# A selective scan on one core: a one-column softplus ahead of the softplus unit's projections, and unit 10 in another order

## The chip, the cores and the metric

The kernel runs on one core of a Trainium2 chip. The metric is the device time of one execution in microseconds, as the median of several runs. The core has five engines that run side by side, each through its own list of instructions in order: TensorE (PE, matmuls and transposes), VectorE (DVE), ScalarE (ACT, activation functions), GpSimd (POOL) and SyncE (SP, which issues most of the DMAs). They wait for one another by semaphores.

## The reference

The input is a batch of 8 images of 384 channels and 64 x 64 points, all fp32. Two layers are added to it one after the other. The first is a channel attention (group norm, 1x1 and 3x3 convolutions, an attention over channels, a projection). The second is a selective scan in four directions; nearly all of the time is spent there:

```python
xs = _cross_scan(x)                                   # 4 directions
x_dbl = jnp.einsum('bkdl,kcd->bkcl', xs, x_proj_weight)
dts, Bs, Cs = (x_dbl[:, :, :R], x_dbl[:, :, R:R + N], x_dbl[:, :, R + N:])
dts = jnp.einsum('bkrl,kdr->bkdl', dts, dt_projs_weight)
dt = jax.nn.softplus(dts + dt_projs_bias[None, :, :, None])
# for every position l, with 384 channels and N = 16 states:
dA = jnp.exp(dtt[..., None] * A)
h = h * dA + (dtt * ut)[..., None] * bt[:, :, None, :]
y = jnp.einsum('bkdn,bkn->bkd', h, ct)
```

The four directions' `y` are summed at the place where they belong, and a layer norm and a GELU follow.

## The kernel before

The images run one after the other. In an image the scan is cut into 32 *steps*: direction k (0 to 3) times eight chunks of 512 positions. A step is cut into 12 *units* r = 0 to 11: three blocks j of 128 channels times four groups g of NV = 4 states. So a unit is four scans of 128 channels x 512 positions, one for each state.

What one unit `u` passes through:

- `drive` (line 950, GpSimd): one product `db` of 128 x 2048 for the four states, from the weighted input `w` and the broadcast `B`. Three `db` buffers.
- `decay` (line 938, ScalarE): `da = exp(dt * A)` into PSUM, one for each state. The pool `ps_a` has three buffers under the tag `da`, so a decay has to wait for the scan three places back; the first projection `pd` of a burst (below) takes its turn in the same three.
- `scan` (line 962, VectorE): `h = da * h + db` along the 512 positions, four to a unit.
- `turn` (line 983, TensorE): four transposes of 128 x 128 into one PSUM tile `pt`; a unit has four such groups. The pool `ps_t` has two buffers, shared with two of the projections.
- `keep` (line 989, ScalarE): the copy `hc` of one `pt` to SBUF.
- `add_up` (line 1000, TensorE): four matmuls that sum the states, weighted with C, into `py`.
- `take` (lines 1040 and 1042, VectorE): adds a finished `py` to the sum of the directions, which SyncE then stores.

The order of all these is written out by hand in `unit(u)` (line 1079), and `pin` keeps it: each engine gets its instructions in the order of the calls. The unit's scans run beside the transposes, copies and sums of the unit before it (`o = u - 1`), and two decays of the next unit are made ahead. `turned(lb)`, `scanned(v)`, `kept(lb)`, `added(lb)` are the calls for one quarter of a unit. The quarter 3 of `add_up` is called one unit later (`added(3, o - 1)`).

In unit 9 of every step but the last of an image the next step's step sizes are made. The code calls it `burst`; there are 31 in an image, 248 in all. TensorE makes three projections `pd` (line 904, `step_matmul`), ScalarE takes the softplus of each (line 912, `step_size`), and VectorE spreads C into four tiles (line 889, `spread_c`). Softplus and exp lie in different activation tables, so ScalarE loads a table ahead of the first softplus and another ahead of the next exp. The burst's own order is:

```python
take(s, 0)
pd0 = step_matmul(s + 1, 0)
kept(1)
pd1 = step_matmul(s + 1, 1)
pd2 = step_matmul(s + 1, 2)
added(0)
for j, pd in enumerate((pd0, pd1, pd2)):
    step_size(s + 1, j, pd)
```

Then come the scans 2 and 3, a decay, `spread_c`, `take(s, 1)`, `added(1)`, `turned(2)`, another decay, `kept(2)`, `turned(3)`, `kept(3)`, `added(2)`. In units 10 and 11 the usual order returns. In unit 10 GpSimd also makes the first `w` (line 921, `weigh`) from the new step size.

The SBUF pools of the scan are `wp` (weights and constants) and, laid behind it, `work` (all tiles that turn over: `B`, `db`, `w`, `dt`, `h`, `hc`, `cp`, the sums).

Of the kernel before, what the change touches and what calls it, by code (L numbers as in the profile page):

```python
# [9 lines left out]
F32 = mybir.dt.float32  # L10
AF = mybir.ActivationFunctionType
# [4 lines left out]
P = 128  # L16
# [79 lines left out]
def tile_channel_attention_then_selective_scan(ctx: ExitStack, tc: tile.TileContext, a: dict):  # L96
    nc = tc.nc
# [19 lines left out]
    small = {}  # L117
# [662 lines left out]
    def selective_scan(b, x1, stats1, after):  # L780

        y_d = dram.tile([L, C], F32, tag="yd", bufs=2, name=f"yd{b}")
        with ExitStack() as st:
            wp = st.enter_context(tc.tile_pool(name=f"sw{b}", bufs=1, reuse_waits="tile"))
# [5 lines left out]
            pin = tc.keep_in_program_order  # L790
# [30 lines left out]
            def view(t, k, c):  # L821

                if k % 2 == 0:
                    return t[:, bass.ts(c, CH)].rearrange("p (x y) -> p x y", y=W)
                return t.rearrange("p (h w) -> p w h", w=W)[:, bass.ts(c, CH // H), :]

            def split(t):
                return t.rearrange("p (x y) -> p x y", y=W)
# [63 lines left out]
            def fetch(s, g):  # L892

                bts[s, g] = work.tile([P, NV, CH], F32, tag="B", bufs=NG, name=f"B{b}_{s}_{g}")
                nc.sync.dma_start(
                    bts[s, g], bc_ds[s][NV * g : NV * (g + 1), :].partition_broadcast(P)
                )

            def step_matmul(s, j):

                k = steps[s][0]
                pool, tag = (ps_a, "da") if j == 0 else (ps_t, "t")
                pd = pool.tile([P, CH], F32, tag=tag, name=f"pd{b}_{s}_{j}")
                pin(nc.tensor.matmul(  # L904
                    pd, lhsT=wdt[:, k, bass.ts(j, P)], rhs=xds[s], start=True, stop=True
                ))
                return pd

            def step_size(s, j, pd):
                k = steps[s][0]  # L910
                dts[s, j] = work.tile([P, CH], F32, tag="dt", bufs=4, name=f"dt{b}_{s}_{j}")
                pin(nc.scalar.activation(  # L912
                    dts[s, j], pd, AF.Softplus, bias=small["dt_bias"][:, j, k : k + 1]
                ))

            def weigh(s, j):

                k, c = steps[s][:2]
                eng = nc.vector if s == 0 else nc.gpsimd
                ws[s, j] = work.tile([P, CH], F32, tag="w", bufs=3, name=f"w{b}_{s}_{j}")  # L920
                pin(eng.tensor_mul(split(ws[s, j]), view(x1[j], k, c), split(dts[s, j])))  # L921
# [3 lines left out]
            def place(u):  # L925

                s, r = divmod(u, UN)
                return s, *divmod(r, NG)

            def decay(i):  # L930

                u, v = divmod(i, NV)
                if u >= U:
                    return
                s, j, g = place(u)
                n = NV * g + v
                t = ps_a.tile([P, CH], F32, tag="da", name=f"da{b}_{u}_{v}")
                pin(nc.scalar.activation(  # L938
                    t, dts[s, j], AF.Exp, scale=neg_a[:, j, steps[s][0], n : n + 1]
                ))  # L940
                das[i] = t
# [11 lines left out]
            def scan(u, v):  # L953
                s, j, g = place(u)
                k, c, start, end = steps[s]
                n = NV * g + v
                if v == 0:
                    hs[u] = work.tile([P, CH, NV], F32, tag="h", bufs=3, name=f"h{b}_{u}")
                da, db, h = das.pop(NV * u + v), dbs[u][:, v, :], hs[u][:, :, v]
                if k >= 2:  # L960
                    da, db, h = da[:, ::-1], db[:, ::-1], h[:, ::-1]
                pin(nc.vector.tensor_tensor_scan(  # L962
                    h, da, db, 0.0 if start else carries[s - 1][:, j, n : n + 1],
                    ALU.mult, ALU.add,
                ))
# [12 lines left out]
            def turn(u, lb):  # L978

                t = ps_t.tile([P, NF, P], F32, tag="t", name=f"pt{b}_{u}_{lb}")  # L980
                for f in range(NF):
                    q = NF * lb + f
                    pin(nc.tensor.transpose(t[:, f, :], hs[u][:, bass.ts(q, HP), :].rearrange("p l v -> p (l v)"), ident))  # L983
                pts[u, lb] = t

            def keep(u, lb):

                t = work.tile([P, NF, P], F32, tag="hc", bufs=6, name=f"hc{b}_{u}_{lb}")
                pin(nc.scalar.copy(t, pts.pop((u, lb))))  # L989
                hcs[u, lb] = t  # L990
# [39 lines left out]
            def sum_of(s, j):  # L1030

                sums[s, j] = work.tile([P, NLB, P], F32, tag="ysum", bufs=3, name=f"ys{b}_{s}_{j}")
                if steps[s][0] > 0:
                    move_y(s, j, sums[s, j], False)
# [13 lines left out]
            for j in range(NJ):  # L1048
                step_size(0, j, step_matmul(0, j))
                weigh(0, j)  # L1050
            for g in range(1, NG):
                fetch(0, g)
            mingle_c(0)
# [25 lines left out]
            def unit(u):  # L1079

                o = u - 1
                s, r = divmod(u, UN)
                nxt = s + 1 < S
                last = u == U
                burst = r == 9 and nxt
                i0 = NV * u

                def scanned(v):
                    if not last:
                        scan(u, v)  # L1090

                def turned(lb):
                    if o >= 0:
                        turn(o, lb)

                def kept(lb):
                    if o >= 0:
                        keep(o, lb)

                def added(lb, of=o):  # L1100
                    if of >= 0:
                        add_up(of, lb)

                if r in (2, 6, 10) and not last:
                    sum_of(s, r // 4)
                if not nxt and r in (8, 10) and not last:
                    take(s, (r - 8) // 2)
                if r >= 8 and nxt:
                    fetch(s + 1, r - 8)

                if not last:
                    drive(u + 1)
                if u >= 2:
                    keep_last(u - 2)
                if r == 7 and nxt:
                    mingle_c(s + 1)
                if r == 10 and nxt:
                    weigh(s + 1, 0)
                if 0 < s < S and r in (0, 2):
                    weigh(s, 1 + r // 2)  # L1120

                turned(0)
                scanned(0)
                added(3, o - 1)
                if r == 4 and s > 0 and not last:
                    take(s - 1, 2)
                decay(i0 + 2)
                kept(0)
                turned(1)
                if r == 8 and nxt:  # L1130
                    turn_c(s + 1)
                scanned(1)
                decay(i0 + 3)
                if burst:
                    take(s, 0)
                    pd0 = step_matmul(s + 1, 0)
                    kept(1)
                    pd1 = step_matmul(s + 1, 1)
                    pd2 = step_matmul(s + 1, 2)
                    added(0)  # L1140
                    for j, pd in enumerate((pd0, pd1, pd2)):
                        step_size(s + 1, j, pd)
                    scanned(2)
                    scanned(3)
                    decay(i0 + 4)
                    for g in range(NG):
                        spread_c(s + 1, g)
                    take(s, 1)
                    added(1)
                    turned(2)  # L1150
                    decay(i0 + 5)
                    kept(2)
                    turned(3)
                    kept(3)
                    added(2)
                    return
                kept(1)
                if nxt and r < 4:
                    for i in range(3):
                        project(s + 1, 3 * r + i)  # L1160
                turned(2)
                added(0)
                scanned(2)
                decay(i0 + 4)
                kept(2)
                turned(3)
                added(1)
                if r == 4 and nxt:
                    lay_out(s + 1)
                scanned(3)  # L1170
                decay(i0 + 5)
                kept(3)
                added(2)
# [136 lines left out]
```

## Time and profile before

| | |
|---|---|
| median of 3 runs | 19440.91 us (19436.96 to 19442.3) |
| the profiled execution | 19452.52 us |
| its span, first to last instruction | 19450.7 us |
| TensorE's mean granted clock | 0.958 |
| VectorE busy | 18413.2 us |
| ScalarE busy | 17504.7 us |
| TensorE busy | 17034.3 us |
| GpSimd busy | 16881.1 us |
| a decay `da`, busy | 713 ns, 12288 of them |
| a copy `hc`, busy | 605 ns, 12288 of them |
| a scan `h` with a carry, busy | 1263 ns, 10752 of them |
| a product `db`, busy | 4581 ns, 3072 of them |
| a table load, busy | 1283 ns, 256 ahead of softplus and 256 ahead of exp in line 938 |

A row of the groups is read so: line, engine, operation, output <- inputs, how many; then busy time and the mean of one in ns; then the engine's idle time just before them and what ended it. A row of the waits is: who <- for whom: us in all, how many times, the longest. A row in order of time is: start, length, engine, line, operation, how many in a row, and in brackets the idle time before it and what ended it. Instructions of one engine follow each other a little closer than their lengths, since they overlap at the ends. TensorE's clock is given as a share of full speed; it is either 1 or one half at a time.

### The profile page before, as it was taken

What the parts mean: (1) busy time and instruction counts of PE and PEld (TensorE: products, weight loads), DVE (VectorE), ACT (ScalarE), POOL (GpSimd) and SP (SyncE); (2) the same over time, 40 slices, a digit from 0 to 9 for tenths busy, and PEclk for the clock granted to TensorE, in tenths of its full rate; (3) what the DMA queues carried; (4) which work ended last, traced back from release to release, by engine and by line L of the source; (5) the groups of instructions that cost most, each with busy time, mean ns of one, the idle gap of its engine ahead of it and who ended that gap; (6) DMA issues with size and microseconds to landing.
All of it is one profiled execution on the core that took longest, in us unless ns stands there. A gap on an engine that the chain in (4) does not pass through costs nothing.

```text
span 19450.7 us, 414947 instructions
## 1 busy us (share of the span) xinstructions
PE 17034.3 (88%) x166560; PEld 10177.3 (52%) x166560; DVE 18413.2 (95%) x17526; ACT 17504.7 (90%) x29605; POOL 16881.1 (87%) x7486
## 2 busy tenths in 40 slices
PE   7888888888888888888888888888888888888887
PEld 4555545555455554555545555455554555545554
DVE  8999989999899998999989999899998999989998
ACT  6999979999799997999979999799997999979998
POOL 4999959999599995999959998599985999869997
PEclk9999999999999999999999999999999999999998
DMA  1232332223322232222322322323223222222323
GB/s 57 85 98 98 101 101 81 97 98 102 103 86 92 96 107 98 87 95 93 103 98 87 98 98 96 104 82 97 98 96 108 83 94 97 96 94 89 98 94 120
DMA packets 1204102, 1849.23 MB, mean 95 GB/s; under 512 B 154656, under 2 KB 1019168, under 8 KB 1064960
## 3 DMA queue, kind: packets, MB, share of 16 engines
q1 hardware_dynamic: 1201312, 1822.57, 28.6%
q8 instruction: 1314, 21.53, 0.5%
q14 instruction: 612, 5.01, 0.1%
q10 hardware_dynamic: 864, 0.12, 0.0%
HBM read 1503.58 MB, written 318.77 MB: 94 GB/s over the span
## 4 chain that ended last, share of the span: by engine, by line
ACT 37%; PE 33%; DVE 18%; issue 6%; POOL 4%; DMA 1%; SPq 0%; DVEq 0%; ACTq 0%; POOLq 0%
ACT da L938 15%; PE pt L983 14%; ACT hc L989 14%; DVE h L962 12%; PE py L1000 7%; PE px L847 5%; DVE ac L457 4%; POOL db L950 4%; ACT dt L912 2%; PE pp L603 2%; ACT pr L419 1%; PE pd L904 1%; PE py L1006 1%; ACT L912 1%; ACT L938 1%
## 5 line engine op out<-in xcount | busy, mean ns | idle before, releaser
L950 POOL TENSOR_TENSOR db<-w,B 128x2048 f32<-128x2048 f32 x3072 | 14061.9, 4581 | 464.6 <-DVE h L962 438.7
L962 DVE TENSOR_TENSOR_SCAN h<-da,ca,db 128x512 f32<-128x512 f32 x10752 | 12783.8, 1263 | 296.6 <-ACT da L938 273.8
L938 ACT ACTIVATE da<-dt,neg_a 128x512 f32<-128x512 f32 x12288 | 8748.9, 713 | 33.5 <-DVE h L962 29.8
L983 PE MATMUL pt<-ident,h 128*128 128x128 f32 x49152 | 8097.9, 293 | 699.3 <-DVE h L962 436.3
L989 ACT COPY hc<-pt 128x512 f32<-128x512 f32 x12288 | 7403.7, 605 | 702.8 <-PE pt L983 644.9
L983 PEld LDWEIGHTS pt<-ident,h 128*128 128x128 f32 x49152 | 5432.6, 145 | 3150.4 <-issue 1877.1
L1000 PE MATMUL py<-hc,cp 128*32 128x128 f32 x98304 | 5061.3, 289 | 897.8 <-ACT hc L989 725.8
L1000 PEld LDWEIGHTS py<-hc,cp 128*32 128x32 f32 x98304 | 2043.3, 109 | 3161.1 <-ACT hc L989 1622.4
L962 DVE TENSOR_TENSOR_SCAN h<-da,db 128x512 f32<-128x512 f32 x1536 | 1749.1, 1206 | 102.3 <-ACT da L938 89.9
L426 POOL TENSOR_TENSOR pr<-pr,pr 128x1008 f32<-128x1008 f32 x288 | 673.1, 2337 | 1194.8 <-ACT pr L419 1172.8
L847 PE MATMUL px<-x,wx 128*44 128x128 f32 x6144 | 1212.9, 341 | 82.1 <-DVE cp L889 68.2
L921 POOL TENSOR_TENSOR w<-x,dt 128x512 f32<-128x512 f32 x744 | 1059.8, 1424 | 27.0 <-ACT dt L912 24.9
L847 PEld LDWEIGHTS px<-x,wx 128*44 128x44 f32 x6144 | 683.7, 127 | 409.9 <-issue 235.2
L904 PE MATMUL pd<-xd,wdt 128*128 128x512 f32 x1536 | 729.3, 611 | 155.8 <-DVE h L962 149.7
L432 POOL TENSOR_TENSOR pr<-pr,pr 128x1008 f32<-128x1008 f32 x288 | 574.8, 1996 | 237.0 <-ACT pr L419 173.2
L603 PE MATMUL pp<-v,mT 128*128 128x512 f32 x1152 | 547.1, 623 | 100.1 <-DVE v L462 99.1
L889 DVE TENSOR_TENSOR cp<-quad,pct 128x512 f32<-128x512 f32 x1024 | 628.0, 674 | 0.0
L976 POOL COPY ca<-h 128x4 f32<-128x4 f32 x2688 | 539.0, 201 | 0.0
L912 ACT ACT_TABLE_LOAD x256 | 328.4, 1283 | 226.2 <-PE pd L904 225.2
L904 PEld LDWEIGHTS pd<-xd,wdt 128*128 128x128 f32 x1536 | 271.4, 190 | 462.6 <-issue 235.2
L912 ACT ACTIVATE dt<-pd,dt_bias 128x512 f32<-128x512 f32 x768 | 474.8, 685 | 6.6 <-PE pd L904 2.9
L1042 DVE TENSOR_TENSOR ys<-ys,py 128x512 f32<-128x512 f32 x576 | 383.7, 666 | 34.6 <-PE py L1000 34.6
(335 smaller groups left out, 11320.2 us busy)
## 6 DMA issues: line engine op xcount, KB each, us to landing
B<-bcd SPq DMA_DIRECT2D x1024, 1024.0 KB, 4.8
yd<-ys SPq DMA_DIRECT2D x384, 256.0 KB, 3.3
ys<-yd SPq DMA_DIRECT2D x768, 128.0 KB, 2.8
yd<-ys SPq DMA_DIRECT2D x768, 128.0 KB, 4.3
x<-in_x SPq DMA_DIRECT2D x48, 1024.0 KB, 7.5
x1d<-x SPq DMA_DIRECT2D x192, 256.0 KB, 3.0
ys<-yd SPq DMA_DIRECT2D x192, 256.0 KB, 2.9
fy<-yd SPq DMA_DIRECT2D x128, 384.0 KB, 4.0
```

Of the source, the lines that this page charges most:

```text
L457: pin(nc.vector.scalar_tensor_tensor(o, pre[:, r0 + dy - lo : r1 + dy - lo, x0 + dx : x1_ + dx], weight(t, tap), o, ALU.mult, ALU.add,))
L603: pin(nc.tensor.matmul(pps[m, c], lhsT=fold_of[0][:, j, bass.ts(m, P)], rhs=vs["v"][:, j, bass.ts(c, CH)], start=j == 0, stop=j == NJ - 1,))
L847: pin(nc.tensor.matmul(split(pxs[s][:XR, :])[:, part, :], lhsT=wx[:, j, k, :], rhs=view(x1[j], k, c)[:, part, :], start=i == 0, stop=i == ...
L904: pin(nc.tensor.matmul(pd, lhsT=wdt[:, k, bass.ts(j, P)], rhs=xds[s], start=True, stop=True))
L912: pin(nc.scalar.activation(dts[s, j], pd, AF.Softplus, bias=small["dt_bias"][:, j, k : k + 1]))
L921: pin(eng.tensor_mul(split(ws[s, j]), view(x1[j], k, c), split(dts[s, j])))
L938: pin(nc.scalar.activation(t, dts[s, j], AF.Exp, scale=neg_a[:, j, steps[s][0], n : n + 1]))
L950: pin(eng.tensor_mul(t, w.broadcast_to([P, NV, CH]), bts[s, g]))
L962: pin(nc.vector.tensor_tensor_scan(h, da, db, 0.0 if start else carries[s - 1][:, j, n : n + 1], ALU.mult, ALU.add,))
L983: pin(nc.tensor.transpose(t[:, f, :], hs[u][:, bass.ts(q, HP), :].rearrange("p l v -> p (l v)"), ident))
L989: pin(nc.scalar.copy(t, pts.pop((u, lb))))
L1000: pin(nc.tensor.matmul(py[f * HP : (f + 1) * HP, lb, :], lhsT=cps[s, g][:, q, :], rhs=hc[:, f, :], start=g == lb == 0, stop=g == NG - 1 an ...
```

## The change

The burst gets one more ScalarE instruction: a softplus of one column of the constant `dt_bias`, into a one-column tile `warm` that nothing reads. It stands between the copy 1 and the second projection in the calls, so on ScalarE it is ahead of the three softplus. The tile is taken from the pool `wp`, once for each image.

In unit 10 of every step the fourth decay (`i0 + 3`) is called right behind the third, ahead of the copies 0 and 1. The sum `added(2)` at the end of the burst moves into unit 10, behind its `turned(0)` and ahead of `added(3, o - 1)`, where it is called with `o - 1` and so is still the sum of the same unit.

```diff
@@ -1048,6 +1048,7 @@
                 weigh(0, j)
+            warm = wp.tile([P, 1], F32, name=f"warm{b}")
             for g in range(1, NG):
@@ -1120,21 +1121,27 @@
                 turned(0)
+                if r == 10 and nxt:
+                    added(2, o - 1)
                 scanned(0)
                 added(3, o - 1)
                 if r == 4 and s > 0 and not last:
                     take(s - 1, 2)
                 decay(i0 + 2)
+                if r == 10:
+                    decay(i0 + 3)
                 kept(0)
                 turned(1)
                 if r == 8 and nxt:
                     turn_c(s + 1)
                 scanned(1)
-                decay(i0 + 3)
+                if r != 10:
+                    decay(i0 + 3)
                 if burst:
                     take(s, 0)
                     pd0 = step_matmul(s + 1, 0)
                     kept(1)
+                    pin(nc.scalar.activation(warm, small["dt_bias"][:, 0, 0:1], AF.Softplus))
                     pd1 = step_matmul(s + 1, 1)
                     pd2 = step_matmul(s + 1, 2)
                     added(0)
@@ -1152,7 +1159,6 @@
                     kept(2)
                     turned(3)
                     kept(3)
-                    added(2)
                     return
```

## The prediction

> **What bounds the kernel now.** I read the page first: the busy shares, then the waits, then one step of the scan in order of time.
>
> ```profile
> PE 17034.3 (88%) x166560; PEld 10177.3 (52%) x166560; DVE 18413.2 (95%) x17526; ACT 17504.7 (90%) x29605; POOL 16881.1 (87%) x7486
> ```
>
> and the groups of instructions, where the figure after the second bar is ScalarE's idle time before them:
>
> ```profile
> L912 ACT ACT_TABLE_LOAD x256 | 328.4, 1283 | 226.2 <-PE pd L904 225.2
> ...
> L938 ACT ACT_TABLE_LOAD x256 | 328.4, 1283 | 4.5
> ```
>
> VectorE is at 95%, so what can be won is at most its idle time. The waits say for whom it idles:
>
> ```profile
> POOL db L950 <- DVE h L962: 438.7, 288, 4.6
> ...
> DVE h L962 <- ACT da L938: 363.7, 824, 2.4
> ...
> ACT L912 <- PE pd L904: 225.2, 217, 1.8
> ```
>
> VectorE loses 363.7 us to decays (`da`) that ScalarE has not made yet. There are 8 images x 31 bursts (unit 9 of a step, where the next step's step sizes are made) = 248, so 1.47 us a burst. GpSimd waits for VectorE, not the reverse: it stands one to two units ahead until its three `db` buffers are full. ScalarE idles 225.2 us before the softplus table load, for the first projection. Where in a step this falls is seen in the order of time; this is one burst of a step with direction 0:
>
> ```profile
> 3163.94 0.59 ACT L989 COPY hc<-pt 128x512 f32<-128x512 f32 x1
> 3165.58 1.28 ACT L912 ACT_TABLE_LOAD   x1 [1.05 <-PE pd L904]
> 3166.87 1.84 ACT L912 ACTIVATE dt<-pd,dt_bias 128x512 f32<-128x512 f32 x3
> 3168.73 1.28 ACT L938 ACT_TABLE_LOAD   x1
> 3170.03 1.30 ACT L938 ACTIVATE da<-dt,neg_a 128x512 f32<-128x512 f32 x2
> 3171.27 1.05 ACT L989 COPY hc<-pt 128x512 f32<-128x512 f32 x2
> 3172.22 0.70 ACT L938 ACTIVATE da<-dt,neg_a 128x512 f32<-128x512 f32 x1
> 3172.95 0.59 ACT L989 COPY hc<-pt 128x512 f32<-128x512 f32 x1
> 3173.43 0.70 ACT L938 ACTIVATE da<-dt,neg_a 128x512 f32<-128x512 f32 x1
> 3174.57 0.58 ACT L989 COPY hc<-pt 128x512 f32<-128x512 f32 x1 [0.45 <-PE pt L983]
> ```
> ```profile
> 3169.55 0.68 DVE L1040 COPY ys<-py 128x512 f32<-128x512 f32 x1
> 3170.82 4.81 DVE L962 TENSOR_TENSOR_SCAN h<-da,ca,db 128x512 f32<-128x512 f32 x4 [0.59 <-ACT da L938]
> 3175.84 3.67 DVE L962 TENSOR_TENSOR_SCAN h<-da,ca,db 128x512 f32<-128x512 f32 x3 [0.21 <-issue]
> ```
>
> Counted from the softplus load at 0: the copy before it ends at -1.05, the three softplus run 1.30 to 3.14, the exp load 3.15 to 4.44, the first decay 4.45 to 5.14. VectorE was free at 4.65 and starts the scan at 5.24: 0.59 lost, the same in nearly every burst. More is lost near 8.9 and 10.1, where decays 3 and 4 of unit 10 and after are late: they stand behind copies (`hc`) that wait for TensorE's transposes (`pt`). By position, counted over the 248 bursts in the trace, VectorE loses 145 us at 4 to 6 us after the load, 118 us at 6 to 12, and 104 us later.
>
> The rest of the step shows what the wait costs. Two steps, one without and one with half-clock time of TensorE in it:
>
> ```profile
> 4580.00:4641.40 61.40, 54.77 (x611) 32.00 (x612) 60.74 (x56) 58.26 (x103) 60.83 (x29) 1.00 0.30 97
> 3165.60:3227.80 62.20, 54.74 (x620) 34.14 (x619) 60.91 (x56) 58.89 (x103) 60.01 (x29) 0.97 0.25 85
> ```
>
> (The columns: length; busy PE, weight load, DVE, ACT, POOL; clock; DMA.) VectorE is busy 60.7 to 60.9 us in both, and the length is that plus its idle: 0.6 and 1.3 us. So a microsecond of wait removed shortens the step by one, down to a floor of about 60.9, where GpSimd's own work (60.0 with directions 0 and 2, 60.8 with 1 and 3) comes in.
>
> **The change, part by part.** *The one-column softplus.* It adds 248 ScalarE instructions and no load: in the built order the table load moves from the first softplus to this one, and loses its wait for TensorE. Its price: the 128x3 square roots of line 166 took 204 ns; the bounds are 0.19 (a one-column accumulator read on ScalarE) and 0.69 (a 512-column softplus); I take 0.20, since three columns are next to one. The load now runs -1.03 to 0.25, the small one to 0.45, and the first softplus starts there instead of at 1.30. The second and third wait for their projections: TensorE's last pass of the third ends at 1.63, so with 0.08 us to be seen the third starts at 1.71 instead of 2.45 and ends at 2.40 instead of 3.14. All behind it gains 0.74. In bursts that already have no wait (the 31 of 248 whose load waited 0 to 0.1, mostly the first of a direction) it costs up to 0.2.
>
> A rule speaks against this. The Trainium skill (ScalarE: Activation LUTs, What ACT_TABLE_LOAD costs) gives a switch 1283 ns for the load and some 1380 ns of drain. The load agrees with the row; but the exp load starts 0.02 us after the third softplus ends, and 256 of them have 4.5 us idle in all before them, so the row has no drain. By the rule the early load would run 0.33 to 1.61 and softplus start at 1.81, 0.51 later than now: 248 x 0.51 = 126 us lost. I take the row.
>
> *Decay 3 ahead of the copies in unit 10, and the sum moved.* No instruction is added. Decay 3 needs a PSUM buffer that scan 0 of unit 10 frees: it may wait there, with copies 0 and 1 (unit 9's transposed states) behind it, and TensorE's third transpose group behind copy 0. The moved sum (`py`, four matmuls, 0.35 us of TensorE's issue by the distance 3171.89 to 3172.25 in the trace) no longer stands ahead of unit 9's first transposes. No DMA moves; the orders of VectorE, GpSimd and SyncE stay as they were. The eight last steps of an image get the reordering without a burst; there the copy is at most one scan (1.2 us) late, behind two buffered transposes: nothing.
>
> *Walk after both* (same zero, durations and pitches of the rows): exp load 2.42 to 3.70; decay 0 to 4.40, so scan 0 starts at 4.57 right behind the sum on VectorE (pitch 0.09 under its end): 0.59 gone. Decay 1 to 5.01, two copies to 6.01, decay 2 to 6.60, decay 3 to 7.2 (scan 0 has ended at 5.86, no wait). Scans 2 and 3 are due at 6.95 and 8.13: both ready. Copies 0 and 1 at 7.12 and 7.60 if TensorE is at full clock (its transposes run from 5.57; the second group, behind the moved sum and the next, ends near 7.5). Decay 4 ends at 8.78, scan 4 is due at 9.31: 0.5 to spare.
>
> *TensorE's clock takes part back.* In the trace's clock record, 222 of 248 bursts are followed by half clock for 3.4 or 6.8 us, starting 5.0 to 8.5 after the load, after a TensorE pause of 2.47 us (3.85 to 6.32). After the change the pause lasts from about 3.55 (third softplus earlier) to 5.57: 2.0 us, shorter, so it comes somewhat less often but not never. With half clock from 5.57 on, four transposes take 1.12 instead of 0.66 and four `py` 0.65 instead of 0.43 (both in the trace), the second group ends at 8.9, decay 4 at 10.1: 0.87 lost; with half clock from 6.8 on, nothing. The Trainium skill (TensorE: Matmul & The Clock Gate, Part 1) has the clock decided by a free-running window of 3413 ns; the trace's half-clock starts do lie on one such grid. Then 18 windows are 61.44 us. A burst that lies badly makes a step of 60.85 + 0.87 = 61.7, one that lies well 60.9; the one slides the burst later against the grid, the other earlier, so steps tend to settle near the edge between, at 61.44 on average. By the rule 0.6 us a burst stay; by the rows alone, with a burst anywhere on the grid, about 0.35. I take 0.6, as the trace has runs of steps of 61.43 already.
>
> **Sum.** 363.7 us of wait now; after it 248 x 0.6 = 149: 215 us saved. The profiled execution took 19452.5 us (span 19450.7), 11.6 over the median 19440.9: 0.06%, left out. 19441 - 215 = **19226 us**, -1.1%.
>
> **Rivals.** (1) *The clock stays up*: with a shorter pause and no settling, 0.2 a burst remain: 363.7 - 50 = 314 saved, **19127**. For: 26 bursts have no half clock now. Against: a pause of 2.0 us is still more than half a window. (2) *Half clock nearly always, and early*: 222 bursts keep 0.87 + 0.25 (late waits): 247 stay, 117 saved, **19324**. (3) *No change*: GpSimd takes VectorE's place, **19441**. Against: over the steps it is busy 60.4 us of 62.4, and the floor that I use is above that. (4) *Slower through addresses*: the small tile stands ahead of the scan's work tiles, so in the built program `B`, `db`, `w`, `dt`, `h`, `hc` and the sums lie 32 bytes further, off the 64-byte multiples they had. Were GpSimd's 12 products a step dearer by 5% (4.58 to 4.81 us), it would be busy 60.4 + 2.8 = 63.2 and bound the step: +1 us x 248, **19690**. It decides from 0.15 us (3%) a product on. Against: tiles that lie at 32 now cost the same (softplus to an aligned tile 0.688, line 374's bias to one at 32 0.687; GpSimd's 768-element product at 32 took 1.82, on the line between its 512 at 1.28 and 2048 at 4.58). No row has these very operations at 32.
>
> **How the numbers follow.** Forecast 0.60 (19180 to 19290), (1) 0.14, (2) 0.13, (3) 0.04, (4) 0.09. A range from 19105 to 19350 holds the first three. Faster by over 0.2% (39 us, about what this measurement can tell) 0.87, within it 0.04, slower 0.09.
>
> **What would show it.** Right: the wait for `pd` before the load gone and 248 one-column softplus near 0.2 us; the 0.59 gap before unit 10's first scan gone; the decay wait of VectorE near 150; `db` at 4.58 us as before. Wrong: idle time between copy and load (a drain); a small softplus over 1 us, from where the early load gains nothing; gaps moved to scan 4 or 5; longer products on GpSimd.

## The result and the profile after

The changed kernel takes 19267.62 us (median of 4 runs, 19259.11 to 19273.3) against 19441.6 us before, measured beside it: 174.0 us less, ratio 0.9908 with a 95% interval of 0.9893 to 0.9922. The forecast was 19226 (19180 to 19290). The profiled execution took 19266.71 us (span 19264.9).

First the instructions of the new line of the kernel after (line 1144).

```profile
L1144 ACT ACT_TABLE_LOAD  x248: 1283/1283/1283, 496.5 to 19087.0; - x124
L1144 ACT ACTIVATE warm<-dt_bias x248: 202/203/206, 497.8 to 19088.3; 128x1 f32<-128x1 f32 x124
```

(Here min/median/max of one in ns, then first and last start.) The table load belongs to the small softplus now, and that softplus takes 203 ns. No row shows a wait ahead of either. Three rows of the waits of the kernel after, then the row of the same name as the last of them in the kernel before:

```profile
POOL db L950 <- DVE h L962: 270.7, 244, 4.5
...
DVE h L962 <- ACT da L938: 147.0, 352, 2.1
...
DVE h L962 <- issue: 65.4, 104, 1.1
```
```profile
DVE h L962 <- issue: 16.5, 52, 0.8
```

VectorE's wait for decays fell from 363.7 to 147.0 us, and ScalarE's 225.2 us ahead of the table load are gone from the list (the softplus themselves now wait 22.0 us for projections). But the scans' row "issue" (nothing that the profile shows) had 16.5 us before and has 65.4 now. A decay has ended less than 0.5 us before each of these 104 scans; I take them for the same wait under another name, which the profile does not show outright. One burst of the kernel after in order of time, from the load on:

```profile
3141.43 0.59 ACT L989 COPY hc<-pt 128x512 f32<-128x512 f32 x1
3142.04 1.28 ACT L1144 ACT_TABLE_LOAD   x1
3143.33 0.20 ACT L1144 ACTIVATE warm<-dt_bias 128x1 f32<-128x1 f32 x1
3143.44 2.05 ACT L912 ACTIVATE dt<-pd,dt_bias 128x512 f32<-128x512 f32 x3
3145.51 1.28 ACT L938 ACT_TABLE_LOAD   x1
...
3149.00 1.31 ACT L938 ACTIVATE da<-dt,neg_a 128x512 f32<-128x512 f32 x2
3150.23 0.59 ACT L989 COPY hc<-pt 128x512 f32<-128x512 f32 x1
3151.07 0.59 ACT L989 COPY hc<-pt 128x512 f32<-128x512 f32 x1 [0.25 <-PE pt L983]
```
```profile
3147.03 0.70 DVE L1040 COPY ys<-py 128x512 f32<-128x512 f32 x1
3147.63 7.17 DVE L962 TENSOR_TENSOR_SCAN h<-da,ca,db 128x512 f32<-128x512 f32 x6
3154.96 1.29 DVE L962 TENSOR_TENSOR_SCAN h<-da,ca,db 128x512 f32<-128x512 f32 x1 [0.16 <-ACT da L938]
3156.73 2.46 DVE L962 TENSOR_TENSOR_SCAN h<-da,ca,db 128x512 f32<-128x512 f32 x2 [0.48 <-ACT da L938]
```

The load starts 0.02 us after the copy. The 0.59 us gap behind `ys` has gone: six scans run without a gap where it was four behind a gap. The waits that are left in this burst come in unit 11, behind copies of ScalarE that wait for transposes (`0.25 <-PE pt`). TensorE is then at half clock, as two stretches of the same burst show (length; busy PE, weight load, DVE, ACT, POOL; clock; DMA):

```profile
3148.00:3150.00 2.00, 1.32 (x21) 0.88 (x22) 2.00 (x3) 2.00 (x5) 2.00 (x1) 0.93 0.93 286
3150.00:3152.00 2.00, 2.00 (x12) 1.43 (x16) 2.00 (x3) 1.75 (x4) 1.17 (x2) 0.50 0.66 197
```

Half clock follows a pause of TensorE. The row that ends the pause, in the prediction's burst of the kernel before and in the burst above:

```profile
3171.89 0.43 PE L1000 MATMUL py<-hc,cp 128*32 128x128 f32 x8 [2.47 <-ACT hc L989]
```
```profile
3148.68 0.66 PE L983 MATMUL pt<-ident,h 128*128 128x128 f32 x4 [2.37 <-ACT hc L989]
```

Counted in the clock record, half clock that begins 4 to 10 us after the load follows 199 of the 248 bursts, against 222 before.

### The profile page after: what moved, and what is told of

Its sections match the earlier page's. It is cut to its first block, busy times and chain, and to the rows that moved or that the text cites. A ratio compares the mean times of both kernels' runs of the same rounds, so it can differ in the third digit from the quotient of the medians.

```text
span 19264.9 us, 415195 instructions
## 1 busy us (share of the span) xinstructions
PE 16919.5 (88%) x166560; PEld 10165.1 (53%) x166560; DVE 18369.1 (95%) x17526; ACT 17529.4 (91%) x29853; POOL 16878.7 (88%) x7486
## 4 chain that ended last, share of the span: by engine, by line
ACT 38%; PE 36%; DVE 19%; issue 5%; DMA 1%; POOL 0%; SPq 0%; DVEq 0%; ACTq 0%; POOLq 0%
ACT da L938 17%; ACT hc L989 15%; PE pt L983 14%; DVE h L962 13%; PE py L1000 7%; PE px L847 5%; DVE ac L457 3%; PE pd L904 3%; PE pp L603 2%; ACT pr L419 2%; PE py L1006 1%; ACT L938 1%; ACT dt L912 1%; ACT ac L419 1%; DVE acc L462 1%
## 5 line engine op out<-in xcount | busy, mean ns | idle before, releaser
L950 POOL TENSOR_TENSOR db<-w,B 128x2048 f32<-128x2048 f32 x3072 | 14064.4, 4582 | 296.1 <-DVE h L962 270.7
L1000 PE MATMUL py<-hc,cp 128*32 128x128 f32 x98304 | 4990.3, 288 | 284.5 <-ACT hc L989 115.0
L603 PEld LDWEIGHTS pp<-v,mT 128*128 128x128 f32 x1152 | 219.1, 198 | 358.7 <-issue 232.3
```

Of the source, the lines that this page charges most:

```text
L603: pin(nc.tensor.matmul(pps[m, c], lhsT=fold_of[0][:, j, bass.ts(m, P)], rhs=vs["v"][:, j, bass.ts(c, CH)], start=j == 0, stop=j == NJ - 1,))
L950: pin(eng.tensor_mul(t, w.broadcast_to([P, NV, CH]), bts[s, g]))
L1000: pin(nc.tensor.matmul(py[f * HP : (f + 1) * HP, lb, :], lhsT=cps[s, g][:, q, :], rhs=hc[:, f, :], start=g == lb == 0, stop=g == NG - 1 an ...
```

## The experiments

Each is timed against the kernel before on its own chip; three chips took part in the experiments, and the kernel before had medians of 19430 to 19445 us on them. A step below is the time from one softplus table load to the next; "ordinary" steps leave out those next to a change of direction or beside the work for the next image (144 of them in a run). Medians are in us; the ratio is to the kernel before.

| kernel | median | ratio, 95% interval | half clock after bursts | mean ordinary step |
|---|---|---|---|---|
| before | 19441.6 | 1 | 222 | 62.25 |
| the change | 19267.62 | 0.9908 (0.9893 to 0.9922) | 199 | 61.46 |
| softplus alone | 19250.85 | 0.9897 (0.9883 to 0.9912) | 170 | 61.46 |
| reordering alone | 19412.24 | 0.9984 (0.9976 to 0.9992) | 202 | 62.15 |
| tile of 64 bytes | 19259.83 | 0.9901 (0.9887 to 0.9916) | 205 | 61.45 |
| change + filler | 19066.12 | 0.9802 (0.9785 to 0.9818) | 0 | 60.66 |
| softplus + filler | 19082.23 | 0.9816 (0.9799 to 0.9832) | 0 | 60.76 |
| before + filler | 19217.23 | 0.9884 (0.9869 to 0.9899) | 0 | 61.40 |
| change + short filler | 19154.82 | 0.9859 (0.9844 to 0.9873) | 119 | 61.00 |

### The two parts apart

The softplus alone is the kernel before with two lines; the reordering alone is the changed kernel without them.

```diff
+            warm = wp.tile([P, 1], F32, name=f"warm{b}")
...
                     kept(1)
+                    pin(nc.scalar.activation(warm, small["dt_bias"][:, 0, 0:1], AF.Softplus))
```

> The one-column softplus alone; unit 10 in its old order, the sum back at the burst's end. Theory A (waits removed, and steps that settle on TensorE's clock grid): the 0.59 us gap ahead of unit 10's first scan goes, a step without half clock falls from 61.43 to about 60.8 us, one with it stays near 61.6, so steps gather at 61.44: 150 to 180 us saved, 19260 to 19290. Rival B (waits removed, one for one): 0.59 x 248 = 146 saved, but the later gaps (118 us at 6 to 12 us after the load) all stay and the rest of the measured gain belongs to the reordering: 19295 to 19320.

> Unit 10's order and the moved sum alone, no softplus and no extra tile. The 0.59 gap stays in both theories. Theory A: a step without half clock stays at 61.43, which is as good as 18 windows of 3.413 us, a step with it falls from 62.2 to 61.8 or so; steps drift to the places without half clock and stay there: 80 to 140 saved, 19300 to 19360, and the savings of the two parts alone add up to clearly more than the 174 of both together. Rival B: only what the softplus alone leaves of the 174: 20 to 40 saved, 19400 to 19420, and the two add up to 174.

Softplus alone: 193 us saved, as much as the whole change or a little more (the intervals overlap), and 13 more than theory A allowed; rival B, with 149 at most, misses by more. Reordering alone: 32 us saved. The sum of the two, 225, is more than the 174 of both, as theory A said, but A had 80 to 140 for the reordering, and its reason fails: the reordering by itself did not send the steps to places without half clock (202 bursts with it, ordinary steps of 62.15). Its 32 us are in rival B's range, and beside the softplus it is worth nothing that these runs can tell. Where VectorE's scans wait, in us over the 248 bursts and by the time from the softplus load to the start of the wait, says why:

| us after the load | before | softplus alone | reordering alone | the change |
|---|---|---|---|---|
| 4 to 6 | 145 | 30 | 144 | 27 |
| 6 to 9.7 | 43 | 25 | 0 | 0 |
| 9.7 to 12.2 | 76 | 41 | 99 | 85 |
| 12.2 to 17 | 41 | 43 | 41 | 51 |

The second row is the wait before scan 3 of unit 10, the third the wait before the first scan of unit 11. The early decay 3 does take away the wait before scan 3 (the second row goes to 0, with and without the softplus). It passed only copy 0, since copy 1 stood behind it already; both copies are still ahead of the next decay, and that one is late in its place: the third row grows by 23 and by 44. The wait is handed on by one scan. Beside the softplus it grows by more than was taken away; half clock also came more often there (199 bursts against 170), and no run tells the two apart.

### Addresses

The one-column tile shifts the scan's work tiles by 32 bytes. A tile of 16 columns shifts them by 64.

```diff
-            warm = wp.tile([P, 1], F32, name=f"warm{b}")
+            warm = wp.tile([P, 16], F32, name=f"warm{b}")
...
-pin(nc.scalar.activation(warm, small["dt_bias"][:, 0, 0:1], AF.Softplus))
+pin(nc.scalar.activation(warm[:, 0:1], small["dt_bias"][:, 0, 0:1], AF.Softplus))
```

> The whole change, with a tile of 16 columns in place of one (only its first column is written), so that the scan's work tiles lie at multiples of 64 bytes as before the change. If the 32-byte shift costs nothing (theory): the time of the change, 19268 within 25 us, and a product on GpSimd at 4.58 us. If the shift cost part of the gain (rival): 19240 or less.

19259.83, 8 us from the change and within the 25 that were expected: the shift costs nothing that can be measured. In the kernel after GpSimd's product has 4582 ns, before 4581. The fourth rival is out.

### TensorE's clock

The filler is ten transposes of the identity at the end of the burst, into columns of the bank of C that hold nothing.

```diff
                     kept(3)
+                    for _ in range(10):
+                        pin(nc.tensor.transpose(pcts[s + 1][:, CH - P :], ident, ident))
                     return
```

> The whole change, and ten transposes of the identity on TensorE behind the burst's last transposes, into columns of the spread-C bank that nobody reads; they run once VectorE has spread C, in TensorE's pause of about 2.4 us, and cover some 1.1 us of it. Theory A: TensorE's clock no longer falls to half after most bursts, steps go from 61.44 to the 60.65 us of the bursts without half clock: 0.78 x 200 = 150 to 190 us less than the change, 19080 to 19120. Rival C (half clock is not what leaves the scan waits, or work on TensorE in the pause delays unit 10's transposes): the time of the change or more, 19260 to 19320.

19066.12: 201 us less than the change, without taking away any work, and 14 more than the best that theory A allowed. TensorE in order of time, in one burst:

```profile
3125.83 1.09 PE L983 MATMUL pt<-ident,h 128*128 128x128 f32 x8
3127.80 1.31 PE L1163 MATMUL pct<-ident 128*128 128x128 f32 x10 [0.88 <-DVE cp L889]
3129.30 0.66 PE L983 MATMUL pt<-ident,h 128*128 128x128 f32 x4 [0.18 <-ACT hc L989]
```

The pause of 2.37 us between the two groups of transposes has become 0.88 and 0.18, and no half clock begins 4 to 10 us after a load any more. The mean clock goes from 0.962 to 0.981. Two steps in a row of the kernel with the filler, then two of the changed kernel:

```profile
3122.66:3183.24 60.58, 54.44 (x630) 34.30 (x631) 60.58 (x56) 58.96 (x103) 60.05 (x29) 1.00 0.27 86
3183.24:3243.83 60.59, 54.45 (x630) 34.34 (x631) 60.59 (x56) 58.96 (x103) 60.03 (x29) 1.00 0.26 85
```
```profile
3142.04:3203.50 61.46, 54.50 (x620) 34.18 (x621) 60.82 (x56) 59.05 (x104) 60.02 (x29) 0.97 0.25 82
3203.50:3264.96 61.46, 54.48 (x620) 34.16 (x621) 60.83 (x56) 59.06 (x104) 60.00 (x29) 0.97 0.26 85
```

With the filler VectorE is busy for the whole of these two steps: nothing but its own work is left. Its row of waits for decays over the whole execution:

```profile
DVE h L962 <- ACT da L938: 72.8, 145, 2.3
```

The changed kernel itself has steps to compare with: of its ordinary steps, those without any half clock took 60.63 us on average, those with some 61.60 (before the change 61.48 and 62.38). The filler's steps, nearly all without, are as long as the first kind, which speaks for the clock, and against something else about the burst, as what the filler changes.

> The one-column softplus and the filler on TensorE, without the reordering of unit 10 and with the sum back at the burst's end. With the clock up, does the reordering still bring anything? Theory A (the order of unit 10 mattered only where transposes run at half clock): the same as the softplus, reordering and filler together, 19066 within 20 us. Rival (decay 3 behind two copies is late at full clock too): the 0.2 to 0.3 us gap near 10 us after the load is back, 50 to 75 us more: 19115 to 19140.

This one takes the filler and the softplus without the reordering: 19082.23, 16 us from the kernel with the reordering and so within the 20 that theory A allowed; the intervals overlap. Between 6 and 12.2 us after the load VectorE's scans wait 0.3 us, all 248 bursts together. So at full clock decay 3 is not late in the old order either, once the softplus come early.

> The kernel before with the filler alone: no one-column softplus, old order. Theory A: no half clock, every step near the 61.43 us that steps without half clock took before, against 62.2: 0.75 x 248 = 185 saved, 19255, as much as the change brings. The 0.59 gap stays in nearly all bursts. Rival (the filler delays the sum and unit 9's transposes on TensorE): 19350 or more.

The filler on the kernel before saves 227 us, 40 more than forecast and more than the change brings. The waits of that kernel:

```profile
ACT L912 <- PE pd L904: 228.2, 217, 1.8
POOL db L950 <- DVE h L962: 204.2, 208, 3.8
DVE h L962 <- ACT da L938: 199.2, 356, 2.2
```

The wait ahead of the table load is there as before, and so is the 0.59 gap (145 us of waits at 4 to 6 us); all of the later waits of a burst are gone (0.4 us at 6 to 17 us, from 160). At full clock the softplus is worth 19217 - 19082 = 135 us, or 0.54 a burst: about the gap of 0.59. The rest of its 193 us without the filler came with bursts that lost their half clock (222 to 170).

> The change with four filler transposes in place of ten: 0.44 us of TensorE's 2.4 us pause covered, not 1.1. If a window with some 40% or more of pause brings half clock (26 bursts of the kernel before had none, and lay so that a window held 1.3 us or less of pause), a pause of 0.85 + 1.1 us, split in two by the filler, still trips it in some bursts: 19120 to 19200, steps at 61.44 in part. Rival: any work in the pause is enough, 19066.

Four transposes in place of ten: 19154.82, between the two, with half clock after 119 bursts. So it is not any work in the pause that helps, but how much of it is covered.

The clock records of these runs show how much. In each of the fourteen kernels all half-clock starts lie within 0.04 us of one grid of 3413 ns. Take the stretches of that grid that end 4 to 12 us after a softplus load and have full clock to their end, and count how long TensorE was idle in each (its ends are modelled in the trace):

| TensorE idle in the stretch | stretches | followed by half clock |
|---|---|---|
| under 1.6 us | 4880 | 0 |
| 1.6 to 1.86 us | 388 | 241 |
| over 1.86 us | 1346 | 1346 |

So at this place half clock comes when about half of a stretch is idle, and a pause of 2.4 us is enough when most of it falls into one; where the burst lies against the grid decides. The share that the forecast of the short filler started from, some 40%, was too low. It is not the whole rule: at other places in the steps 18 to 43 stretches of each kernel with less than 1.6 us idle were followed by half clock too, and these runs do not say why.

### Do the steps settle on the clock's grid?

If they do, work added to VectorE is paid only in part. The first pair of kernels puts an instruction of 384 columns into unit 5, without and with the filler.

```diff
+                if r == 5:
+                    pin(nc.vector.tensor_scalar_mul(spare, avg[:, 0, :], 1.0))
                 kept(1)
```

> The whole change and, in unit 5 of every step, one more VectorE instruction of 384 columns (a constant times 1 into a tile that nobody reads), estimated 0.37 to 0.46 us from VectorE's 128-column (0.28) and 512-column (0.54) rows; 256 of them. If steps settle on TensorE's clock grid, at 18 windows of 3.413 us = 61.44, a step without half clock goes from 60.65 to 61.05, which is still under 61.44, so the mean stays where it is: +0 to +45 us, 19268 to 19313. If there is no settling: the full 95 to 118 us, 19363 to 19386.

> The same added VectorE instruction on the change with the filler, where no burst has half clock and so no grid. Both theories: the full price, 95 to 118 us over 19066: 19161 to 19184. Much less would say that VectorE is not what bounds the step, and would take the meaning from the same kernel without the filler.

20104.22 and 19977.14: 837 and 911 us more, eight times the estimate, so the pair says nothing about the grid. In the second kernel the instruction takes 4256 ns in the median. VectorE and GpSimd there, in order of time:

```profile
2025.24 4.66 DVE L1167 TENSOR_SCALAR spare<-avg 128x384 f32<-128x384 f32 x1
```
```profile
2025.10 4.55 POOL L950 TENSOR_TENSOR db<-w,B 128x2048 f32<-128x2048 f32 x1
```

It ends 0.25 us after the product that runs on GpSimd; of the 212 that took over 1 us all end 0.2 to 0.35 us after a product. The Trainium skill (SBUF — State Buffer, Who interferes with whom) has VectorE and GpSimd share one pair of SBUF ports under an exclusive lock, which some VectorE forms need; these ends, right behind the product's, agree with it. So the second pair takes a form that reads its data from PSUM, the burst's last spread of C, made a second time with the same values at the end of unit 11.

```diff
                 scanned(3)
+                if r == 11 and nxt:
+                    for _ in range(1):
+                        spread_again(s + 1)
                 decay(i0 + 5)
```

> The added VectorE work again, now an instruction that reads one input from PSUM: the burst's last spread of C (0.68 us, 0.60 from start to start) is made a second time at the end of unit 11, with the same values; 248 of them, on the whole change. If steps settle on TensorE's clock grid at 61.44, a step without half clock goes from 60.65 to 61.25, still under it, and the mean stays: +0 to +50 us, 19268 to 19318. Rival, no settling: 0.60 x 248 = +149 us, 19417, or some 40 less where the work covers a scan's wait for its decay.

> The same one more spread on the change with the filler, where no burst is followed by half clock. Both theories: the full 149 us over 19066, 19215; it prices the instruction where nothing settles.

> Two more spreads a step on the whole change (1.2 us). A step without half clock is then at 61.85, above 61.44, so it cannot settle there: with the grid theory the second spread costs much more than the first, +120 to +220 us over the run with one (with half clock more often or less as the phase falls). Rival, no settling: the second costs what the first did.

| added | on the change | on the change + filler |
|---|---|---|
| nothing | 19267.62, 0.9908 | 19066.12, 0.9802 |
| one spread | 19283.49, 0.9923 (0.9907 to 0.9940) | 19163.41, 0.9863 (0.9849 to 0.9878) |
| two spreads | 19506.72, 1.0036 (1.0023 to 1.0049) | |

The first spread costs 16 us (29 by the ratios) where half clock is about, and 97 (119 by the ratios) where it is not. The forecast for the latter, 149, was too high: most steps are longer by the 0.6 of the instruction, but those around a change of direction take it in for nothing. The second spread costs 223, just over the 120 to 220 of the grid theory. No fixed price of the instruction gives 16 and then 223. With one spread half clock follows 120 of the bursts, with two 159, with none 199: with the first, fewer slow bursts set off most of its cost. So adding to a step does change how many bursts run into half clock. That steps *settle* at 61.44 is not shown. In the changed kernel 60 of 144 ordinary steps lie within 0.06 us of it (15 before, none with change and filler). But with one more spread it is 6, and the ordinary steps of that profile average about 61.7 instead of staying; with the softplus alone it is 13, at the same mean of 61.46; and on the kernel before with the filler it is over 60 again, where no burst is followed by half clock. What decides where the steps stay is open.

## Why the prediction was right

The time lies in the forecast's range and the mechanism held for the softplus. For the size of the saving it was helped by luck, as the sum below shows.

**The small softplus: right.** 203 ns against 0.20. From the first projection's start to the end of the third softplus it was 4.35 us before and is 3.62 now, 0.73 less against 0.74. The row without a drain decided rightly against the rule: the load starts 0.02 us after the copy.

**The gap ahead of unit 10's first scan: right.** 145 us at 4 to 6 us after the load have become 27.

**The reordering: the walk was right, its worth was not.** Decay 3 is in time, and at full clock the six scans follow each other as walked. But the old order does that too at full clock, and at half clock the wait only moves to the next decay: the gap moved to scan 4, which the prediction had named as a sign of being wrong, did come (76 us to 85). The walk put both parts together and never walked the softplus alone. That would have shown it: with its own figures decay 2 ends at 6.60, copy 0 at about 7.1 and decay 3 at about 7.7, and scan 3 is due at 8.13.

**The clock: right in kind.** Half clock is what makes the decays of units 10 and 11 late, as the fillers show. The pause that I had at 2.0 us is 2.37: counted from where the load stood before, it ends at 5.60 as walked (5.57), but begins at 3.22 instead of 3.55, and half clock comes nearly as often as before.

**The sum: its waits were mis-sized, and a gain that it had not counted makes up part of that.** 0.6 us of wait a burst were to remain, 149 in all, and the row of 147.0 seems to say so. But with the renamed 65.4 and three small ones (16.7, 8.5, 1.6) the rows of VectorE's scan waits add up to 239 us, from 387 before: 148 saved, not 215, and 0.96 a burst stayed. The wait in the stretch that was walked, up to 12.2 us after the load, fell from 265 us to 112, or 0.45 a burst, which is between the two estimates of 0.35 and 0.6. What the sum put at nothing is the wait that the prediction itself had counted later than that, 104 us, and some 30 outside the bursts' steps: it took the whole 363.7 as if all but 0.6 a burst could be won, and these two are 107 and 30 after the change (gaps too short for the rows of waits counted in). In return VectorE's busy time fell by 44.1 us (18413.2 to 18369.1), since scans that follow without a gap overlap at their ends, and the prediction had not counted that. 148 + 44 is 192 in all, against 186 between the two spans. Without the 44 the waits alone would have made about 19293, just outside the range of 19180 to 19290. By the profiles the steps gained 195 us, and what lies outside them lost 9.

**The rivals.** The clock staying up, 19127, is what the filler brings about (19066) and the change doesn't. Half clock nearly always and early, 19324, was nearer than 19127, but too high. GpSimd did not become the bound, and the addresses cost nothing.

**A version that beats both**: the change with the filler, 19066.12 us, ratio 0.9802 (0.9785 to 0.9818) to the kernel before and 1.0% under the change.

## What to carry to other kernels

Before moving instructions about to hide a wait, ask what makes the thing that is waited for slow: here it was in large part TensorE's clock after a pause of 2.4 us in each step, and on the kernel before ten empty transposes in that pause were worth more than the change (227 us against 174). Walk each part of a change alone as well as together, since a part that looks right in the sum may only hand a wait to the next instruction. And where some steps run into half clock and some don't, added work is not paid for in proportion (here 16 us, then 223); price an edit where the clock is steady. When a sum takes a wait from a row of the whole execution, take out first what lies where the change doesn't reach.

## What the runs showed of the hardware that was not expected

- Half clock follows TensorE pauses that are shorter than the 3.413 us between the places where it can start: 2.47 us before the change (222 of 248 bursts), 2.37 after it (199). With the pause cut to 0.88 and 0.18 it never came there; with four filler transposes it came in 119. What counts there is how much of one stretch of the 3.413 us grid is idle: under 1.6 us never, over 1.86 always.
- A 384-column fp32 `TENSOR_SCALAR` on VectorE, from SBUF to SBUF, took 331 to 5821 ns beside GpSimd's products, 4256 in the median; the 512-column products with an input in PSUM (the spreads of C, in the kernels with one and two more of them) took 0.65 to 0.69 us.
- A switch of ScalarE's table costs its 1283 ns and 0.01 to 0.02 us on either side; no drain is to be seen at the small softplus or at the exp behind the softplus.
